# Rounding by conversion to int16 and int8, and a last batch without transfers, in a cross-attention and ternary-FFN kernel

## The chip, the cores and the metric

The kernel runs on one core of one Trainium2 chip. The metric is the device time of one execution in microseconds (us); lower is better. The kernel before is given by the median of 3 executions, and one further execution was recorded by the hardware profiler.

## The reference

The inputs are x and a context, both 32 x 128 x 512 in float32. One layer of cross attention (8 heads of 16 channels over 512 positions, with rotary embedding on half of each head) is followed by a feed-forward part (FFN) whose weights are rounded to three values and whose activations are rounded to 8 bits:

```python
def act_quant(x):                      # per token
    scale = 128 / clip(max(abs(x), axis=-1), 1e-5)
    return clip(round(x * scale), -128, 127) / scale

def weight_quant(w):                   # one scale for the whole matrix
    scale = 1.0 / clip(mean(abs(w)), 1e-5)
    return clip(round(w * scale), -1, 1) / scale

x = x + Wo @ attention(layernorm(x), ctx)          # softmax(q k / 4) v
h = layernorm(x)
z = silu(act_quant(h) @ weight_quant(w_gate).T) * (act_quant(h) @ weight_quant(w_up).T)
x = x + act_quant(fwht(z)) @ weight_quant(w_down).T  # fwht: Walsh-Hadamard over 2048
```

## The kernel before

One batch is a tile of 128 channels by 512. The 32 batches run through a software pipeline, each through these steps (the name of the step, then what it issues):

- `load`, `a`, `a2`, `a3`, `v`: x and the context come in; layer norm; projections to q, k and v on PE; the rotary part on GpSimd (POOL); q and k go through DRAM (`xd`) into the layout of the scores, `qs` and `ks` (`st`).
- `mpe`, `mdve`, `mfin`: a first product of q and k (L642, into the PSUM tile `pS`), whose row maxima are taken on VectorE (DVE, L657), transposed, and written into spare rows of `qs`.
- `epe`, `eact`, `eav`: the second, transposed product with the maxima inside it (L712, `pT`), its exponential on ScalarE (ACT, L725), and the product with v (L746, `pav`). The v tile has 16 columns of ones beside each head's 16, so `pav` holds each head's 16 outputs and 16 copies of its softmax sum.
- `u`, `o`: `pav` is copied by ACT (L769) and written to DRAM (`ud`); the sums (`sc`) and outputs (`N`) are read back, the reciprocals are made (L800), written (`rd`) and read back spread out (`RB`); N times RB (L812), the output projection (L821) and the residual (L825) give `x1`.
- `o2`: layer norm of x1, its absolute maximum, rounding to 8 bits, and a transposing DMA into `xqT` (L864).
- `gpe`, `gact`, `upe`, `udve`: gate and up products in fp8 weights (L880), SiLU (L910), product (L935).
- `bf`, `zt`, `hi`, `lo`, `hm`, `yv`: four Walsh-Hadamard stages on POOL or DVE (L964), transposes on PE (L984), and the last stages as products with a 128 x 128 Hadamard matrix in two parts (L1023, L1024), copied into `y` (L1038).
- `am`, `q`, `q1`, `q2`, `dn`: maxima of y (L1051), scaling (L1099), rounding (L1109, L1123), and the down product (L1141), the result being added to x1 (L1147) and written out.

The weights are rounded at the start by the steps `w` to `w4`: each of the three matrices comes in four tiles of 128 x 2048; absolute sums on ACT or DVE (L367), then scaling (L391), clipping (L401) and conversion to fp8 (L409). All rounding is done by adding and subtracting the constant 12582912 (`MAGIC`) in float32. For the down product, L1123 writes 127 minus the rounded value, so that a clip at zero is a clip at 127; a column sum of the weights (L418) and one more matmul of two rows (L1142, from `NEG` and `CS`) take the offset out again. The gates of the first batch wait for all twelve weight tiles (mark `wr` 2).

The order of the instructions on each engine is not written by hand. Every step is a Python generator that yields what it needs: a buffer of a ring (`get`), a mark of another step (`on`), or an engine with a planned duration. The class `Plan` plays all generators against each other when the program is built and issues, among those that can start earliest, the one of lowest rank: a number for each step in the table `CFG`, plus `T` times the batch. Where a step names two engines (as L964 does), `Plan` takes the one that ends first, with a handicap `pen` for the second. `RINGS` says how many buffers each tile has (`x1` 4, `pf` 3, `pS` and `pT` one each). On the chip each engine then runs its list in order.

Of the kernel before, what the change touches and what calls it, by code (L numbers as in the profile page):

```python
# [10 lines left out]
F32 = mybir.dt.float32  # L11
FR = mybir.dt.float32r
BF = mybir.dt.bfloat16
F8 = mybir.dt.float8e4
AF = mybir.ActivationFunctionType
# [5 lines left out]
MAGIC = 12582912.0  # L21
# [4 lines left out]
    "a": 17040.0,  # L26
    "a2": 9587.6,
    "a3": 24145.2,
    "am": 15370.4,
    "bf": 32443.0,  # L30
    "const": -13702.6,
    "dn": -12954.6,
    "eact": -26357.5,
    "eav": 10024.8,
    "epe": -25661.6,
    "gact": 12255.9,
    "gpe": 25689.6,
    "hi": 17693.4,
    "hm": -13331.7,
    "init": -13147.7,  # L40
    "lo": 14260.1,
    "load": -14103.3,
    "mdve": -26910.2,
    "mfin": -15116.6,
    "mpe": -17532.8,
    "o": -16894.5,
    "o2": -35355.2,
    "q": 9579.7,
    "q1": 31393.3,
    "q2": 30321.2,  # L50
    "st": -39068.5,
    "u": 12892.7,
    "udve": -12899.7,
    "upe": 40468.8,
    "v": 41001.5,
    "w": 11036.2,
    "w1": 23901.9,
    "w2": 38371.3,
    "w3": 34207.9,
    "w4": 33907.2,  # L60
    "yv": -12466.7,
    "zt": 12210.4,
    "T": 69.4,
    "eps": 0.025,
    "pen": 8.4,
    "stick": 7462.1,
    "epspe": 0.214,
# [5 lines left out]
    "xq": 1, "xqT": 2, "pf": 3, "z0": 2, "z1": 1, "hl": 2, "y": 1, "yq": 2, "ot": 1,  # L73
# [3 lines left out]
class Plan:  # L77

# [16 lines left out]
    def __init__(self, nc, rings, cfg):  # L95
        self.nc = nc
        self.free = dict.fromkeys(("pe", "act", "dve", "pool", "sp", "dma"), 0.0)
        self.port = {"dve": 0.0, "pool": 0.0}
        self.slots = {k: [0.0] * n for k, n in rings.items()}
        self.marks = {}  # L100
        self.tasks = []
        self.cfg = cfg
        self.now = 0.0
        self.done = 0.0
        self.eng = None
        self.table = None
        self.mode = 0
        self.locked = False
        self.tail = 0
# [11 lines left out]
    def step(self, t):  # L121
        self.now = max(t[1], t[7] + self.LAT[t[6]]) if t[6] else t[1]
        while True:
# [10 lines left out]
            t[0] = self.cfg[t[4]] + self.cfg["T"] * r[1]  # L134
# [45 lines left out]
    def run(self):  # L180
        for t in list(self.tasks):
            self.step(t)
        while True:
# [4 lines left out]
            for t in self.tasks:  # L188
# [5 lines left out]
                elif isinstance(r[0], tuple):  # L194
                    f = [(self.start(t, e), e, d) for e, d in zip(*r[:2])]
                    pen = self.cfg["pen"] if t[5] < self.tail else 0.0
# [29 lines left out]
def xattn_ffn(  # L226
# [37 lines left out]
    MAG = const.tile([128, 1], F32, name="MAG")  # L264
    nc.vector.memset(MAG, MAGIC)
    NMAG = const.tile([128, 1], F32, name="NMAG")
    nc.vector.memset(NMAG, -MAGIC)
    MAG7 = const.tile([128, 1], F32, name="MAG7")
    nc.vector.memset(MAG7, MAGIC + 127.0)
# [10 lines left out]
    CW = const.tile([128, 388], F32, name="CW")  # L280
    WQ, WK, WVT, BRP, MASK = CW[:, 0:128], CW[:, 128:256], CW[:, 256:384], CW[:, 384:386], CW[:, 386:387]
    NEGC = CW[:, 387:388]
    CM = const.tile([128, 386], F32, name="CM")
    EYE, WOT, HADF, BVO = CM[:, 0:128], CM[:, 128:256], CM[:, 256:384], CM[:, 384:386]
    ROPE = const.tile([128, 2, T], F32, name="ROPE")
    COS, SIN = ROPE[:, 0, :], ROPE[:, 1, :]
    HAD = const.tile([128, 128], FR, name="HAD")
    BO = const.tile([128, 1], F32, name="BO")
# [8 lines left out]
    ob = const.tile([128, 1], BF, name="ob")  # L297
    nc.vector.memset(ob, 1.0)
    NEG = const.tile([2, 128], BF, name="NEG")
    CS = const.tile([2, 512], BF, name="CS")  # L300

    p = Plan(nc, RINGS, CFG)
    p.tail = NB - 2
    st = [dict() for _ in range(NB)]
    NU = 2 * NB
    EARLY = 6

    def s_const():
# [6 lines left out]
        nc.scalar.copy(HAD, HADF)  # L315
        p.mark("had")
# [9 lines left out]
    def s_init():  # L326
        yield "on", "cw"
        yield "dve", 0.2
        nc.vector.tensor_scalar(NEG, ones[0:2, :], NEGC[0:2], None, ALU.mult)
# [15 lines left out]
    WR = ("z0", "z1", "z0", "y")  # L345

    def s_w():
        for n in range(12):
            m, k = divmod(n, 4)
            src = srcs[m][0][k]  # L350
            yield "get", WR[n % 4]
            yield "dma", 2.9
            w = fp.tile([128, 2048], F32, name=WR[n % 4], bufs=2 if WR[n % 4] == "z0" else 1)
            nc.sync.dma_start(out=w.rearrange("p (j i) -> p j i", j=4) if m == 2 else w, in_=src)
            WT[n] = w
            p.marks["w", n] = p.done
            p.now = p.done - 2.9

    def s_w1():
        for m in range(3):  # L360
            for n in range(4 * m, 4 * m + 4):
                yield "on", "w", n
                for h in range(2):
                    yield ("act", "dve"), (1.1, 1.13)
                    w, a = WT[n][:, bass.ts(h, 1024)], acc[:, 2 * n + h : 2 * n + h + 1]
                    if p.eng == "act":
                        nc.scalar.activation(AB, w, AF.Abs, accum_out=a)  # L367
                    else:
                        nc.vector.tensor_reduce(a, w, AX.X, ALU.add, apply_absolute_value=True)
            yield "get", "pf"  # L370
            yield "pe", 0.1
            pw = ps_f.tile([128, 512], F32, name="pf")
            nc.tensor.matmul(pw[:, 0:8], ones, acc[:, 8 * m : 8 * m + 8], start=True, stop=True)
            yield "dve", 0.1
            sw = SW[:, m : m + 1]
            nc.vector.tensor_reduce(sw, pw[:, 0:8], AX.X, ALU.add)
            p.put("pf")
            yield "dve", 0.1
            nc.vector.tensor_scalar(sw, sw, 1.0 / (NI * 128 * 512), EPS, ALU.mult, ALU.max)
            yield "dve", 0.1  # L380
            nc.vector.reciprocal(SC[:, m : m + 1], sw)
            p.mark("sw", m)

    def s_w2():
        for n in range(12):
            m = n // 4
            yield "on", "sw", m
            yield ("act", "pool", "dve"), (1.95, 2.7, 1.25), "port"
            w = WT[n]
            if p.eng == "act":  # L390
                nc.scalar.activation(w, w, AF.Identity, bias=MAG, scale=SC[:, m : m + 1])  # L391
            else:
                E[p.eng].tensor_scalar(w, w, SC[:, m : m + 1], MAGIC, ALU.mult, ALU.add)
            p.mark("w2", n)

    def s_w3():
        for n in range(12):
            yield "on", "w2", n
            yield ("dve", "pool"), (1.2, 2.7), "port"
            w = WT[n]  # L400
            E[p.eng].tensor_scalar(w, w, MAGIC - 1.0, MAGIC + 1.0, ALU.max, ALU.min)  # L401
            p.mark("w3", n)

    def s_w4():
        for n in range(12):
            m, k = divmod(n, 4)
            yield "on", "w3", n
            yield "act", 1.95
            nc.scalar.activation(srcs[m][1][:, k, :], WT.pop(n), AF.Identity, bias=NMAG, saturate=False)  # L409
            p.put(WR[n % 4])  # L410
            if k == 3:
                p.mark("wr", m)
        yield "get", "y"
        yield "get", "pf"
        yield "pe", 3.5
        pc = ps_f.tile([128, 512], F32, name="pf")
        for j in range(NI):
            nc.tensor.matmul(pc[0:1, :], ob, WDQ[:, j, :], start=(j == 0), stop=(j == NI - 1))  # L418
        yield "dve", 0.6
        w = fp.tile([128, 2048], F32, name="y")  # L420
        ca, cb = w[0:1, 0:512], w[0:1, 512:1024].bitcast(BF).rearrange("p (a f) -> p a f", a=2)
        nc.vector.tensor_scalar(ca, pc[0:1, :], 1.0 / 64.0, MAGIC, ALU.mult, ALU.add)
        yield "dve", 0.6, "port"
        nc.vector.tensor_scalar(cb[:, 0], ca, -MAGIC, None, ALU.add)
        yield "dve", 0.6, "port"
        nc.vector.tensor_scalar(ca, ca, -MAGIC, -64.0, ALU.add, ALU.mult)
        yield "dve", 0.6
        nc.vector.tensor_tensor(cb[:, 1], pc[0:1, :], ca, ALU.add)
        p.put("pf")
        yield "dma", 0.1  # L430
        nc.sync.dma_start(out=CS, in_=cb)
        p.now = p.done
        p.put("y")
        p.mark("cs")
# [324 lines left out]
    def s_u():  # L759
        for u in range(NU):  # L760
# [3 lines left out]
            yield "get", "U"  # L764
            yield "act", 0.48
# [10 lines left out]

    def s_o():
        for b in range(NB):
            s = st[b]
            yield "at", b  # L780
            yield "get", "xr"
            yield "on", "ud", 2 * b + 1
# [40 lines left out]
            yield "dve", 0.66  # L823
            x1 = x1p.tile([128, T], F32, name="x1")
            nc.vector.scalar_tensor_tensor(x1, po, BO, xr, ALU.add, ALU.add)  # L825
            p.put("pf")
            p.put("xr")
            s["x1"] = x1
            p.mark("x1", b)

    def s_o2():
        for b in range(NB):
# [18 lines left out]
            yield "get", "pf"  # L851
            yield "act", 0.75
            w = ps_f.tile([128, 512], F32, name="pf")
            nc.scalar.activation(w, l2, AF.Identity, bias=MAG, scale=sx)
            yield "dve", 0.6
            xq = xp.tile([128, T], BF, name="xq", bufs=1)
            nc.vector.tensor_scalar(xq, w, -MAGIC, 127.0, ALU.add, ALU.min)
            p.put("pf")
            p.put("l2")
# [358 lines left out]
```

## Time and profile before

| | |
|---|---|
| median of 3 executions | 1450.17 us (1441.77 to 1455.94) |
| the profiled execution | 1449.79 us, of which the span is 1447.9 us |
| granted PE clock, mean over the span | 0.950 |
| POOL L964, x489 | 616.7 us busy, 1283 ns each |
| DVE L657, x488 | 595.1 us busy, 1219 ns each |
| ACT L725, x512 | 523.0 us busy, 1022 ns each |
| PE L1142, x32 | 12.3 us busy, 384 ns each |

The profile is one execution. For each engine it gives the time in which at least one instruction was in work; matmuls are pipelined, so a busy PE need not be at its peak. The span is also cut into stretches, with the busy time of each engine and the mean clock that was granted to PE (1.00 is full). "Idle before" names what ended the idle time ahead of an instruction.

### The profile page before, as it was taken

The page shows a single profiled execution, that of the slowest core. Times are in us where ns is not written, and L with a number is a line of the kernel's source. Part 1 is how long each engine was busy: PE and PEld are TensorE (multiplying, and loading weights), DVE is VectorE, ACT ScalarE, POOL GpSimd, SP SyncE. Part 2 cuts the span into 40 slices and gives each one's busy share as a digit, 9 for nine tenths or more (in the row PEclk, how much of TensorE's full clock was granted, in tenths as well). Part 3 has the DMA queues.
Part 4 walks back from the last instruction along what each step waited for, and adds up shares of the span by engine and source line. Part 5 has one row for each costly group of instructions (what it writes and reads, how often), then busy time and mean ns, then how long its engine had stood idle before and what let it go on. Part 6 is the DMA issues. An engine that isn't in the chain of part 4 may idle for free.

```text
span 1447.9 us, 21862 instructions
## 1 busy us (share of the span) xinstructions
PE 1354.9 (94%) x7448; PEld 529.9 (37%) x7448; DVE 1173.9 (81%) x1755; ACT 1192.3 (82%) x1575; POOL 990.2 (68%) x778
## 2 busy tenths in 40 slices
PE   3797799999999999999999999999999999999965
PEld 1222233333334343333334433334333434433322
DVE  2975878888888888888888888888889888886565
ACT  5778977888988888888888888888888888888743
POOL 3112319987777878877777787887777777777830
PEclk7567999999999999999999999999999999999986
DMA  8948745454456565555445556555544555321100
GB/s 284 294 145 270 220 110 159 145 145 117 150 157 173 166 175 166 155 151 149 118 153 161 170 170 174 167 153 147 144 129 149 163 170 155 94 72 43 41 26 14
DMA packets 137699, 215.23 MB, mean 149 GB/s; under 512 B 37618, under 2 KB 39924, under 8 KB 136564
## 3 DMA queue, kind: packets, MB, share of 16 engines
q1 hardware_dynamic: 137588, 213.84, 50.4%
q8 instruction: 59, 0.97, 0.3%
q14 instruction: 52, 0.43, 0.1%
HBM read 107.35 MB, written 93.85 MB: 139 GB/s over the span
## 4 chain that ended last, share of the span: by engine, by line
PE 77%; POOL 7%; DVE 6%; ACT 5%; DMA 3%; issue 2%; SPq 0%; POOLq 0%; ACTq 0%; DVEq 0%
PE pav L746 16%; PE pf L880 13%; PE pT L712 13%; PE pS L642 9%; PE pf L1141 8%; POOL z L964 4%; PE pf L472 4%; PE pf L984 4%; PE pf L1023 3%; ACT P L725 2%; PE pf L821 2%; PE pf L552 2%; PE pf L1024 2%; DVE M L657 2%; POOL N L812 1%
## 5 line engine op out<-in xcount | busy, mean ns | idle before, releaser
L964 POOL TENSOR_TENSOR z<-z 128x512 f32<-128x512 f32 x489 | 616.7, 1283 | 103.0 <-DVE z L935 60.7
L657 DVE TENSOR_REDUCE M<-pS 128x2 f32<-128x1024 f32 x488 | 595.1, 1219 | 90.6 <-PE pS L642 89.1
L725 ACT ACTIVATE P<-pT 128x1024 f32<-128x1024 f32 x512 | 523.0, 1022 | 145.6 <-PE pT L712 144.0
L746 PE MATMUL pav<-P,va 128*32 128x512 f32 x2048 | 281.8, 623 | 0.0
L712 PE MATMUL pT<-qs,ks 50*128 50x512 f32 x1024 | 260.1, 504 | 20.8 <-ACT P L725 18.7
L642 PE MATMUL pS<-ks,qs 48*128 48x512 f32 x976 | 227.5, 457 | 12.3 <-DVE M L657 7.5
L712 PEld LDWEIGHTS pT<-qs,ks 50*128 50x128 f32 x1024 | 97.8, 187 | 242.2 <-ACT P L725 144.0
L448 POOL TENSOR_TENSOR arstd<-arstd,MHALF 128x1 f32<-128x1 f32 x32 | 18.5, 579 | 195.6 <-DVE arstd L445 160.5
L880 PEld LDWEIGHTS <-xqT 128*128 128x128 bf16 x1024 | 91.8, 99 | 155.3 <-issue 83.2
L1099 POOL TENSOR_TENSOR y<-y,YB 128x1024 f32<-128x1024 f32 x60 | 140.9, 2369 | 9.0 <-ACT YB L1085 9.0
L1141 PE MATMUL pf<-WDQ,yq 128*128 128x512 fp8e4 x512 | 127.9, 396 | 16.3 <-ACT yq L1123 16.3
L1051 DVE TENSOR_REDUCE ya<-y 128x128 f32<-128x1024 f32 x64 | 127.3, 1989 | 12.9 <-ACT y L1038 12.6
L642 PEld LDWEIGHTS pS<-ks,qs 48*128 48x128 f32 x976 | 95.9, 190 | 112.8 <-issue 43.5
L880 PE MATMUL pf<-WGQ,xqT 128*128 128x512 fp8e4 x512 | 131.4, 382 | 0.9 <-DVE ot L1147 0.5
L880 PE MATMUL pf<-WUQ,xqT 128*128 128x512 fp8e4 x512 | 126.8, 381 | 0.5 <-DVE X L525 0.2
L935 DVE TENSOR_TENSOR z<-z,pf 128x512 f32<-128x512 f32 x128 | 84.3, 675 | 17.2 <-PE pf L880 13.7
L996 ACT CAST hi<-pf 128x512 fp32r<-128x512 f32 x128 | 74.1, 586 | 26.8 <-PE pf L984 26.7
L910 ACT ACTIVATE z<-pf,tk 128x512 f32<-128x512 f32 x128 | 84.1, 684 | 8.0 <-PE pf L880 4.7
L1007 DVE TENSOR_TENSOR lo<-pf,hi 128x512 fp32r<-128x512 f32 x128 | 85.5, 675 | 3.0 <-ACT hi L996 3.0
L1141 PEld LDWEIGHTS <-yq 128*128 128x128 bf16 x512 | 46.7, 101 | 99.3 <-ACT yq L1123 27.4
L984 PE MATMUL pf<-CM,z 128*128 128x128 f32 x512 | 82.2, 285 | 0.8 <-DVE z L964 0.4
L1038 ACT COPY y<-pf 128x512 f32<-128x512 f32 x128 | 71.7, 584 | 9.5 <-PE pf L1024 9.4
(118 smaller groups left out, 1780.0 us busy)
## 6 DMA issues: line engine op xcount, KB each, us to landing
xd<-X SPq DMA_DIRECT2D x128, 512.0 KB
qs<-xd SPq DMA_DIRECT2D x128, 192.0 KB
ks<-xd SPq DMA_DIRECT2D x128, 192.0 KB
ud<-U SPq DMA_DIRECT2D x64, 256.0 KB
xt<-x SPq DMA_DIRECT2D x32, 256.0 KB
ct<-cx SPq DMA_DIRECT2D x32, 256.0 KB
RR<-R SPq DMA_DIRECT2D x64, 128.0 KB
N<-ud SPq DMA_DIRECT2D x32, 256.0 KB
```

The costliest lines, as they stand in the source:

```text
L642: nc.tensor.matmul(ps[e], qs[w, t, bass.ts(qt, 128)], ks[w, t, :], start=True, stop=True)
L657: nc.vector.tensor_reduce(m, ps[2], AX.X, ALU.max)
L712: nc.tensor.matmul(ps[:, e], ks[w, t, bass.ts(kt, 128)], qs[w, t, :], start=True, stop=True)
L725: nc.scalar.activation(P, TQ[u, n], AF.Exp, scale=0.25)
L746: nc.tensor.matmul(av[32 * h : 32 * h + 32, :], va[:, kt, 4 * hf + h, :], P[:, e], start=(kt == 0), stop=(kt == 3),)
L880: nc.tensor.matmul(ps, xqT[:, k, :], W[:, k, bass.ts(c, 512)], start=(k == 0), stop=(k == 3))
L964: E[p.eng].tensor_tensor(ix(dv, k), ix(av, 0), ix(av, 1), o)
L984: nc.tensor.transpose(ps[:, i, :], st[b]["z"][:, bass.ts(4 * c + i, 128)], EYE)
L1007: nc.vector.tensor_tensor(t, F.pop(("z", b, c)), F["hi", b, c].bitcast(F32), ALU.subtract)
L1051: nc.vector.tensor_reduce(ya[:, h], s["y"][:, 8 * h : 8 * h + 8].rearrange("p j t -> p t j"), AX.X, ALU.max, apply_absolute_value=True,)
L1099: E[p.eng].tensor_tensor(y, y, st[b]["YB"].to_broadcast([128, 8, 128]), ALU.mult)
L1141: nc.tensor.matmul(ps, s["yq"][:, j, :], WDQ[:, j, :], start=(j == 0), stop=False)
```

## The change

1. **Rounding by conversion.** A value is written to an int16 tile (activations) or int8 tile (weights), which rounds it. x: ACT writes `xi` (int16), DVE takes the minimum with 127 into bf16. y: ACT copies y into `yi` (int16), and `q2` moves from ACT to DVE, where it takes the minimum with 127. The offset of 127 goes, and with it `NEG`, `CS`, the column sum and the matmul L1142. Weights: scaling into int8 (POOL, ACT or DVE; in the built program all 14 are on POOL), then one clip on DVE that writes fp8; the steps on ACT (L391, L409) and the separate clip (L401) go.
2. **Weights in another order.** Gate and up weights first, in 10 pieces; the gates of the first batch wait for these alone (`wr` 1). The down weights come through the tile `y` one by one, twice: once for the sum, once for the rounding (8 transfers of 1 MB instead of 4). The first `dn` waits for them.
3. **The last batch** (`SHORT`). `u` takes the reciprocal of `pav` on DVE, moves it by a shuffle within groups of 32 partitions onto the outputs, and multiplies, with no DRAM; `o` is two matmuls with a padded weight `WOZ`. x is transposed by four matmuls with a bf16 identity and an ACT copy, in place of the DMA.
4. **The order.** `CFG` holds three numbers for each step, for the first 4 batches (`.h`), the last 4 (`.z`) and the rest, with new values; `pen` 42.9 instead of 8.4, `T` 295.0 instead of 69.4, `stick` 14510 instead of 7462. So all engines' lists are in a new order.

```diff
-            t[0] = self.cfg[t[4]] + self.cfg["T"] * r[1]
+            part = ".h" if r[1] < self.head else ".z" if r[1] >= self.tail else ""
+            t[0] = self.cfg.get(t[4] + part, self.cfg[t[4]]) + self.cfg["T"] * r[1]
...
+    def w_scale(w, wi, m):
+        f = w.shape[1] / 2048
+        yield ("pool", "act", "dve"), (2.6 * f + 0.1, 1.85 * f + 0.1, 1.15 * f + 0.1), "port"
+        if p.eng == "act":
+            nc.scalar.activation(wi, w, AF.Identity, scale=SC[:, m : m + 1])
+        else:
+            E[p.eng].tensor_scalar(wi, w, SC[:, m : m + 1], None, ALU.mult)
+    def w_clip(wi, o):
+        yield "dve", 1.1 * wi.shape[1] / 2048 + 0.15, "port"
+        nc.vector.tensor_scalar(o, wi, 1.0, -1.0, ALU.min, ALU.max, saturate=False)
...
+    def s_wd():
+        yield "on", "st", 1
+        for n in range(8):
+            ph, k = divmod(n, 4)
+            yield "get", "y"
+            yield "dma", 2.9
+            w = fp.tile([128, 2048], F32, name="y", bufs=1)
...
@@ s_u
+            if b in SHORT:
...
+                nc.vector.reciprocal(U, av)
...
+                nc.vector.stream_shuffle(RB, U, SWAP)
...
+                nc.vector.tensor_tensor(U, av, RB, ALU.mult)
...
@@ s_o
+                for hf in range(2):
+                    nc.tensor.matmul(po, WOZ[:, bass.ts(hf, 128)], s["U", hf], start=(hf == 0), stop=(hf == 1))
...
@@ s_o2
-            nc.scalar.activation(w, l2, AF.Identity, bias=MAG, scale=sx)
-            nc.vector.tensor_scalar(xq, w, -MAGIC, 127.0, ALU.add, ALU.min)
+            nc.scalar.activation(xi, l2, AF.Identity, scale=sx)
+            nc.vector.tensor_scalar(xq, xi, 127.0, None, ALU.min)
...
+                    nc.tensor.matmul(pt[:, k, :], xq[:, bass.ts(k, 128)], EYEB, start=True, stop=True)
...
+                nc.scalar.copy(xqT, pt)
...
@@ s_q1, s_q2, s_dn
-                nc.scalar.activation(y, y, AF.Identity, bias=MAG)
+                nc.scalar.copy(st[b]["yi"][:, w], st[b]["y"][:, w])
...
-                yield "act", 1.05
+                yield "dve", 0.42, "port"
...
-                nc.scalar.activation(s["yq"][:, w], s["y"][:, w], AF.Relu, bias=MAG7, scale=-1.0)
+                nc.vector.tensor_scalar(s["yq"][:, w], s["yi"][:, w], 127.0, None, ALU.min)
...
-            nc.tensor.matmul(ps, NEG, CS, start=False, stop=True)
```

How far the steps stand from each other is part of the change too, and can be read from the lists of the two built programs. When PE's list comes to the first L712 of batch 28, the kernel before has 26 batches of gates and 23.5 of `dn` behind it, the changed one 24 and 21. After the last L712, PE has 207 matmuls left before, 360 after. Where PE goes over from a matmul of the full array to one of half its rows (L642, L712), the list before does so 417 times, the changed one 345 times; the number of ways back (half to another form) is 568 and 570. One such turn and its price are worked out below.

## The prediction, made blind

> **What bounds the kernel now.** I read first the busy times and the clock over the span, then stretches cut at the first L712 of batches 0, 1, 2, 3, 4, 5 and 27 and at the last one, then the timeline of one steady stretch and of the end. In the page's rows the reader is to see that PE is full except at both ends, and that its clock is low in the same places:
>
> ```profile
> PE 1354.9 (94%) x7448; PEld 529.9 (37%) x7448; DVE 1173.9 (81%) x1755; ACT 1192.3 (82%) x1575; POOL 990.2 (68%) x778
> ...
> PEclk7567999999999999999999999999999999999986
> ```
>
> The stretches (us; busy PE, weight load, DVE, ACT, POOL with counts; granted clock; DMA share; GB/s) say who is full where:
>
> ```profile
> 61.00:105.00 44.00, 40.66 (x167) 13.08 (x166) 32.13 (x48) 30.52 (x37) 6.89 (x6) 0.58 0.55 186
> 105.00:145.00 40.00, 31.07 (x158) 9.37 (x154) 22.75 (x33) 35.66 (x44) 7.36 (x7) 0.79 0.83 264
> 145.00:184.00 39.00, 30.23 (x164) 10.04 (x164) 32.21 (x47) 38.60 (x42) 13.35 (x11) 0.95 0.74 217
> 184.00:233.00 49.00, 47.41 (x242) 16.26 (x242) 36.67 (x54) 34.28 (x40) 17.40 (x16) 0.94 0.38 99
> 272.00:1161.00 889.00, 886.70 (x5116) 349.31 (x5112) 774.84 (x1147) 769.10 (x1036) 708.86 (x554) 1.00 0.54 155
> 1360.00:1448.00 88.00, 56.07 (x216) 24.76 (x214) 54.40 (x91) 41.39 (x59) 25.02 (x17) 0.80 0.08 26
> ```
>
> From 272 to 1161 us (22 batches, 40.4 us each) PE is busy 99.7%: the body costs what PE's list costs. DVE is at 87%, ACT 87%, POOL 80%. From 105 to 184 ACT is the full engine (74.3 of 79 us). The last 88 us are nobody's: PE 64%, DVE 62%.
>
> **PE's list (term A).** A turn and the matmul L1142 can be priced in the timeline (start, length, engine, line):
>
> ```profile
> 712.94 1.90 PE L1141 MATMUL pf<-WDQ,yq 128*128 128x512 fp8e4 x8
> ...
> 714.77 0.50 PE L712 MATMUL pT<-qs,ks 50*128 50x512 f32 x2
> ...
> 720.40 1.90 PE L1141 MATMUL pf<-WDQ,yq 128*128 128x512 fp8e4 x8
> ...
> 722.24 0.38 PE L1142 MATMUL pf<-CS,NEG 2*128 2x512 bf16 x1
> ...
> 722.55 0.50 PE L712 MATMUL pT<-qs,ks 50*128 50x512 f32 x2
> ```
>
> Eight L1141 and then L712 take 1.83 us from start to start; with L1142 between, 2.15. So one L1142 is worth 0.32 us, 32 of them 10.2. The column sum L418 is 16 matmuls of 0.22 (their starts): 3.5, and it goes too. A turn from the full array to half of it: four L880 take 0.87 from their start to that of another full matmul (704.47 to 705.34) and 0.96 to that of L712 (700.16 to 701.12), so 0.09; the new list has 417 - 345 = 72 fewer, 6.5. The last batch adds four small matmuls and one L821 (two passes): about 1.3. A = 10.2 + 3.5 + 6.5 - 1.3 = 19 us less, nearly all of it where PE is the bound. For whole stretches I price the list by the median time between the starts of one kind of matmul and the next kind, taken between 290 and 1300 us: a body batch then costs 39.9 us, and took 40.4.
>
> **The steps moved to DVE.** Per batch DVE loses L857 (0.68) and gets two `q2` of 128x1024 and one minimum of 128x512 out of int16. No row of before reads int16. The bounds: L424, float32 to bf16 within SBUF, takes 0.41 for 512; L422, the same size out of PSUM, 0.68. So 1024 elements cost between 0.41 (should 16-bit input again halve L424's time per element) and 1.22 (L657's length for 1024). I take 0.41 to 0.68, near L424, because source and target lie in SBUF. DVE then gains 0.4 to 1.1 us a batch on the 35.2 that it has now (774.8 over 22); PE's list needs 39.5 after A's body part (0.5). DVE stays at 90 to 92%: no loss, and no gain. ACT loses L1123 (2 x 1.14) and is at 80%. The Trainium skill (VectorE: DVE Perf Modes, "The perf-mode tier table") gives 16-bit tensor-scalar work in SBUF four results per cycle and float32 two; by it the 1024 elements would be an estimated 0.43 us, and DVE's gain the lower one. No row here has shown it for int16.
>
> What speaks against it is POOL:
>
> ```profile
> 32.78 1.23 DVE L401 TENSOR_SCALAR z<-z 128x2048 f32<-128x2048 f32 x1 [2.16 <-ACT z L391]
> 32.94 2.19 POOL L580 TENSOR_TENSOR R<-R,RR 128x512 f32<-128x512 f32 x1
> ```
>
> L580 takes 1.31 on average; begun just behind a DVE L401 it took 2.19, so the DVE operation held it up for about 0.9. If each new DVE operation does the same for its whole length, POOL gets 1.1 to 1.8 us a batch on its 32.2 (708.9 over 22): 34 of 39.5. It fits, so I price it at nothing; the cover is POOL's 20% of idle time. The Trainium skill (SBUF: State Buffer, "Who interferes with whom") states the rule that this row obeys: a DVE operation in a two-port mode and a POOL operation never run together, the second one waits for the whole first. By it these operations cost POOL their full length, the case just priced.
>
> **The head (term B).** L391 and L409 take 12 x 2.09 + 12 x 2.0 = 49 us from ACT; 12 of these 24 (24.6 us) start within 105 to 184, where ACT is full. POOL gets the scaling instead: 12 tiles' worth at 2.1 (four times the memset L275 of 512, 0.53) to 4.7 us (L1099's rate, 2.37 for 1024), 25 to 57 us, in a stretch where POOL is busy 45 of 172 us (61 to 233); it queues ahead of the rotary work (L575 to L585), which feeds later batches and is not late. The gates of batch 0 no longer wait for the down weights. Four more 1 MB loads queue on SP among DMAs busy 74 to 83%. If ACT was the bound, up to 24.6 us go; if PE at its low clock is (0.58 from 61 to 105, with PE busy 92%), none. What is late next is PE: its busy time in 105 to 184, weighted by the clock, is 31.1 x 0.79 + 30.2 x 0.95 = 53 us of 79. I take 12, half of the bound.
>
> **The end (term C).** Batch 31 before, in the timeline:
>
> ```profile
> 1365.30 0.59 ACT L769 COPY U<-pav 128x512 f32<-128x512 f32 x1
> ...
> 1384.85 0.75 DVE L825 SCALAR_TENSOR_TENSOR x<-pf,BO,xr 128x512 f32<-128x512 f32 x1
> ...
> 1393.09 1.22 SPq L864 DMA_TRANSPOSE xqT<-xq  x1
> ...
> 1399.59 0.59 PE L880 MATMUL pf<-WGQ,xqT 128*128 128x512 fp8e4 x2 [0.51 <-DVE ot L1147]
> ```
>
> From `pav` to L825 it is 19.5 us, by way of DRAM. The new way is a reciprocal, a shuffle and a product, then two matmuls of two passes. The reciprocal L800 takes 0.33 for 32 elements and its form with one element 0.16, so 5.4 ns for each more: up to 2.9 us for 512, and no less than the 0.68 of other 512-element rows; I take 2.9, the same operation. With 0.7 + 0.7 + 1.9 for the rest that makes 6.2: 13 less. xqT: 6.5 us from issue to the gates, against four matmuls and an ACT copy, 0.4 + 0.59 and handovers: 5 less. So 18 us off the last batch's chain. How much of it counts? By the price of the list, PE's work behind the last L712 is 43 us before, in 88: 45 lost. The new list leaves 75 us behind it (32 shifted from the body, neutral in the sum), so there is more work to cover the chain; but that work is also DVE's and POOL's, 7 batches' `dn` with their L1051 and L964. Both bounds are open: 0 if DVE and POOL set the end, 25 if the cover is full. I take 17, the chain.
>
> **The sum.** 1449.8 (the profiled execution; the median, 1450.2, is the same) - 19 - 12 - 17 = 1402 us.
>
> **Rivals.**
> 1. *The list alone.* The head is bound by PE's low clock and the end by DVE and POOL: only A counts, 1431. For it: clock 0.58 with PE busy 92%. Against: ACT at 38.60 of 39.
> 2. *The new order stalls.* PE's list before repeats 187 matmuls with 42 turns in every batch of the body; the new one varies between 155 and 215. Of the 40.4 us 0.5 is stalls today. At 1.5, 28 more: with B and C 1430, without them 1459, which is no change.
> 3. *Slower: DVE becomes the bound.* If reading int16 runs at one element per cycle, `q2` costs 1.22, the minimum 0.68: DVE 35.2 + 2.4 = 37.6 of 39.5, 95%. Its list is strict, and L657, which frees `pS` for PE, queues behind each `q2` that waits for ACT's L1257. It decides from about 1.0 us per `q2`, where DVE passes 94%. If DVE can't be driven above 90%, a batch takes 41.8, 1.4 more than now, 39 us in 28 batches, and nothing of A but L418, nor of C, is left: 1450 - 3.5 - 12 + 39 = 1474.
>
> That the short way is not taken is excluded: the new lists hold it, once.
>
> **Chances.** A, B and C together 0.6; rival 1 0.15; rival 2 0.15 (a third of it with the gains); rival 3 0.1. What a measurement of this kernel can tell from no change is about 1%, 14.5 us. Faster by more: 0.6 + 0.15 + 0.05 = 0.80; within it 0.11; slower 0.09. The range: the full bounds of B and C (24.6 and 25) give 1381, and 9 more if the body's stalls go, 1372; upwards it takes rival 1 and stalls of 0.3 a batch more, 1440.
>
> **What would show it.** PE in the body must stay above 99% with no L1142; a body batch near 39.5 of PE's list; the length of `q2` between 0.41 and 0.68; the start of the fifth batch's L712 near 208 instead of 233 (13 of it because one batch's gates and ups, 7, half a batch of L642, 2.7, and L418, 3.5, come later or not at all); the stretch behind the last L712 near 100 us instead of 88, with PE's 75 in it. I am wrong if DVE or POOL fills the body, if a POOL scaling takes over 5 us and holds up `qs` and `ks`, or if the end takes 115.

## The result and the profile after

The changed kernel takes 1516.78 us (median; 1516.06 to 1521.76), the kernel before 1446.94 beside it: 1.048 times, 95% interval 1.042 to 1.055. 1402 was forecast, and faster. The profiled execution took 1521.76 us, its span is 1520.0.

The page's rows of the changed kernel that answer to the two shown of before:

```profile
PE 1369.6 (90%) x7406; PEld 545.8 (36%) x7406; DVE 1234.7 (81%) x1815; ACT 1082.1 (71%) x1483; POOL 1073.2 (71%) x795
...
PEclk7567979999999999999999999999999999989977
```

PE has 42 matmuls less and is busy 15 us longer in a span that is 72 us longer. ACT has lost 110 us of work, DVE and POOL have 61 and 83 more, and none of the three is above 81%. No engine has become full.

The stretches of the changed kernel, cut at its own first L809 (the old L712) of batch 5 and of batch 27 and at the last one (columns as before: stretch, length, busy PE, weight load, DVE, ACT, POOL, clock, DMA share, GB/s):

```profile
274.00:1168.00 894.00, 866.77 (x4946) 345.11 (x4945) 780.29 (x1140) 703.67 (x956) 667.75 (x518) 1.00 0.51 150
1168.00:1386.00 218.00, 204.39 (x1079) 83.10 (x1077) 171.37 (x247) 159.74 (x215) 163.73 (x124) 0.95 0.30 90
1386.00:1520.00 134.00, 91.48 (x370) 43.42 (x368) 95.31 (x157) 53.93 (x87) 77.87 (x55) 0.83 0.07 22
```

The first of these stretches is called the body here, the last one the end. In the body PE was idle for 2.3 us of 889; now it is for 27 of 894. The end has 134 us for 88, with 91 of PE in them for 56. What PE waited for in the body (engine, tile and line, what it waited for; us in all, times, longest), changed kernel:

```profile
PE pS L739 <- DVE M L754: 10.3, 21, 1.4
PE pT L809 <- ACT P L822: 9.5, 21, 1.1
```

Before, the only such row was this:

```profile
PE pf L821 <- POOL N L812: 2.1, 4, 1.0
```

Now PE comes to the scores before DVE or ACT has emptied the one buffer of `pS` or `pT`.

Priced as in the prediction, PE's list has 881 us of work between the first L712 of batch 5 and that of batch 27 before, and took 889; the new one has 840 (FFN work has been put off until later) and took 894. By this estimate stalls of 8 us have become 54, 2.45 a batch; 27 of the 54 are PE's idle time above, the other 27 lie within its busy time (867 us for a list of 840). The whole list became 16 us shorter, from 1279 to 1263, where term A had 19; the time lost beside it went from 169 to 257 us. In the table, the last column counts the gate matmuls (16 a batch) that are still to come after the last scores:

| first scores of batch (us) | 0 | 4 | 5 | 27 | last | end | gate matmuls left |
|---|---|---|---|---|---|---|---|
| before | 61 | 233 | 272 | 1161 | 1360 | 1448 | 28 |
| changed | 70 | 225 | 274 | 1168 | 1386 | 1520 | 60 |

So of 72 us, 2 had been lost at batch 5, 7 at batch 27, 26 at the last scores, and 46 come behind them. In the stretch from batch 27 to the last scores the granted clock fell as well. Before, it was 1.00 there:

```profile
1161.00:1360.00 199.00, 193.91 (x1075) 78.59 (x1071) 156.21 (x231) 168.28 (x224) 153.50 (x118) 1.00 0.36 100
```

Now it is 0.95, and about as many matmuls (1079) keep PE busy for 204 us instead of 194; that is half of the 19 us lost there. No run separates this from the stalls that come with it.

The end is not idle for want of one engine. Its chain (start, length, piece; changed kernel) lies on POOL from 1410.66 to 1428.86, and then hands the work round between ACT, PE, DVE and POOL:

```profile
1432.63 0.72 ACT xi L987
1433.98 2.76 PE pf L1024 x12
1436.77 0.69 DVE z L1079
1441.14 2.36 POOL y L1243
1443.52 1.05 ACT yi L1257
1444.60 1.48 DVE yq L1274
1446.13 3.59 PE pf L1292 x8
```

Three costs could lie behind the whole loss: the operations put on DVE, which wait for POOL; the weights' scaling on POOL; and the order. The groups of the changed kernel (busy us, mean ns of one):

```profile
L1274 DVE TENSOR_SCALAR yq<-yi 128x1024 bf16<-128x1024 int16 x64 | 54.2, 859 | 18.5 <-ACT yi L1257 18.4
L991 DVE TENSOR_SCALAR xq<-xi 128x512 bf16<-128x512 int16 x32 | 22.1, 691 | 2.1 <-ACT xi L987 2.1
...
L867 DVE RECIPROCAL U<-pav 128x512 f32<-128x512 f32 x2 | 6.7, 3358 | 2.5 <-PE pav L843 2.5
L870 DVE STREAM_SHUFFLE RB<-U 128x512 f32<-128x512 f32 x2 | 1.5, 737 | 0.0
```

The mean of L1274 hides two kinds. In the timeline of the changed kernel, the first here has POOL idle, and the pair below begins while POOL is in L1108:

```profile
627.75 0.42 DVE L1274 TENSOR_SCALAR yq<-yi 128x1024 bf16<-128x1024 int16 x1
...
739.11 4.12 POOL L1108 TENSOR_TENSOR z<-z 128x512 f32<-128x512 f32 x3
...
739.43 2.67 DVE L1274 TENSOR_SCALAR yq<-yi 128x1024 bf16<-128x1024 int16 x2
...
742.02 1.21 DVE L754 TENSOR_REDUCE M<-pS 128x2 f32<-128x1024 f32 x1
```

The 12 that began with POOL idle took 0.418 us on average (0.40 to 0.43). The 52 with a POOL operation in flight took 0.96, up to 1.61, and most ended 0.28 to 0.29 us after that operation. This waiting of a DVE operation for a POOL operation in flight is called the lock below. L754, which empties `pS`, stands behind them.

### The profile page after: what moved, and what is told of

It reads as the page before. It is cut to its first block, busy times and chain, and to the rows that moved or that the text cites. A ratio compares the mean times of both kernels' runs of the same rounds, so it can differ in the third digit from the quotient of the medians.

```text
span 1520.0 us, 21799 instructions
## 1 busy us (share of the span) xinstructions
PE 1369.6 (90%) x7406; PEld 545.8 (36%) x7406; DVE 1234.7 (81%) x1815; ACT 1082.1 (71%) x1483; POOL 1073.2 (71%) x795
## 4 chain that ended last, share of the span: by engine, by line
PE 52%; DVE 22%; POOL 7%; DMA 7%; ACT 7%; issue 5%; SPq 1%; ACTq 0%; POOLq 0%; DVEq 0%
PE pav L843 10%; PE pf L1024 10%; PE pT L809 9%; DVE M L754 8%; PE pS L739 7%; PE pf L1292 6%; ACT P L822 4%; DVE ya L1195 3%; PE pf L569 2%; POOL yi L466 2%; POOL z L1108 2%; PE pf L1128 2%; DMA xd<-X 2%; DVE yq L1274 2%; PE pf L961 2%
## 5 line engine op out<-in xcount | busy, mean ns | idle before, releaser
L1108 POOL TENSOR_TENSOR z<-z 128x512 f32<-128x512 f32 x491 | 624.4, 1293 | 106.1 <-DVE z L1079 72.0
L754 DVE TENSOR_REDUCE M<-pS 128x2 f32<-128x1024 f32 x488 | 594.7, 1219 | 118.5 <-PE pS L739 116.4
L809 PE MATMUL pT<-qs,ks 50*128 50x512 f32 x1024 | 260.5, 505 | 36.4 <-ACT P L822 35.4
L843 PE MATMUL pav<-P,va 128*32 128x512 f32 x2048 | 286.3, 629 | 1.9 <-ACT U L882 1.6
L739 PE MATMUL pS<-ks,qs 48*128 48x512 f32 x976 | 233.6, 470 | 43.2 <-DVE M L754 32.5
L809 PEld LDWEIGHTS pT<-qs,ks 50*128 50x128 f32 x1024 | 99.0, 190 | 289.4 <-ACT P L822 187.6
L1243 POOL TENSOR_TENSOR y<-y,YB 128x1024 f32<-128x1024 f32 x60 | 140.9, 2371 | 52.8 <-ACT YB L1229 52.8
L569 PE MATMUL pf<-ct,CW 128*32 128x512 f32 x256 | 77.0, 674 | 1.4 <-DVE lo L1151 1.2
L1128 PE MATMUL pf<-CM,z 128*128 128x128 f32 x512 | 78.2, 284 | 0.1
```

The lines of the kernel that those rows point to most:

```text
L569: nc.tensor.matmul(ps[64 * dh + 32 : 64 * dh + 64, :], WK[:, w], ct, start=True, stop=True)
L739: nc.tensor.matmul(ps[e], qs[w, t, bass.ts(qt, 128)], ks[w, t, :], start=True, stop=True)
L754: nc.vector.tensor_reduce(m, ps[2], AX.X, ALU.max)
L809: nc.tensor.matmul(ps[:, e], ks[w, t, bass.ts(kt, 128)], qs[w, t, :], start=True, stop=True)
L843: nc.tensor.matmul(av[32 * h : 32 * h + 32, :], va[:, kt, 4 * hf + h, :], P[:, e], start=(kt == 0), stop=(kt == 3),)
L1108: E[p.eng].tensor_tensor(ix(dv, k), ix(av, 0), ix(av, 1), o)
```

## The experiments

Each changes the kernel named. Ratios are to the kernel before, measured on the same chip, with their 95% intervals; it took 1446 to 1449 us on each of them, so times of different runs are also set side by side. "Order kept" means that every engine's list is the same but for the operations named. In the expectations, "order theory" lays the loss on the new lists whatever the operations are, and "operations theory" on the new operations whatever the order is.

**e1, e2: ranks and program crossed.**

```diff
e1, changed kernel:   CFG, T, pen, stick: those of before
e2, kernel before:    CFG, T, pen, stick, the .h and .z ranks: those of the changed kernel
```

> The changed kernel (int16/int8 rounding, last batch without transfers) with the step ranks, T, pen and stick of the kernel before; the ranks have no separate values for the first and last batches. If the new order is the cause (PE stalls of 2 us a batch in the body and 134 us behind the last pT product), this falls back to 1400 to 1440 us, with the body at 40 us a batch or less and under 100 us behind the last pT product. If the rounding steps on DVE, which wait for POOL, are the cause, it stays above 1480. If both, 1440 to 1480.

> The kernel before (rounding by a large constant, offset matmul, last batch through DRAM) with the step ranks, T, pen and stick of the changed kernel, separate for the first 4 and last 4 batches. If the order is the cause: 1490 us or more, again with a body of unequal batches and a long end. If the rounding is the cause: 1430 to 1460. If the order suits only the durations it was made for, it is slower than both.

1538.9 (1.061, 1.054 to 1.068) and 1544.9 (1.066, 1.060 to 1.071). Both bodies take 42.0 us a batch, both ends over 125 us. Neither set of ranks belongs to the old or the new rounding as such; a set gives a good list only with the program and the planned durations it stands with, and these two runs do not yet tell order from operations.

**e3: without the short way.**

```diff
-    SHORT = (NB - 1,)
+    SHORT = ()
```

> The changed kernel with the last batch through DRAM and the transposing DMA like all others. If the short way shortens the end as I priced it: 10 to 18 us slower than the changed kernel, 1527 to 1535. If DVE and POOL set the end, within 5 us of it, 1512 to 1522. If the two 3.36 us reciprocals hurt, faster by up to 7.

1514.4 (1.045, 1.031 to 1.058): part 3 of the change brings nothing that can be measured. The interval, of two executions, is as wide as the gain that was forecast; in the profiled execution the end takes 132 us without the short way, against 134 with it.

**e4: the minima taken out, order kept.** It leaves out the rounding and clipping of x and y: ACT writes bf16, and each minimum is cut to one element per partition.

```diff
-                nc.vector.tensor_scalar(s["yq"][:, w], s["yi"][:, w], 127.0, None, ALU.min)
+                nc.vector.tensor_scalar(s["yq"][:, w, 0:1], s["yq"][:, w, 0:1], 127.0, None, ALU.min)
```

> The changed kernel in exactly its order on every engine, but ACT writes x and y as bf16 without rounding and the DVE minima with 127 shrink to one element a partition (activations are not rounded; the weights are). This takes 76 us of DVE time away. If the waits of these minima for POOL, and the time they hold DVE, are the cause: the body falls to 38.5 to 39.3 us a batch and the whole to 1440 to 1475. If the order is the cause whatever DVE does: above 1500.

1501.9 (1.036, 1.032 to 1.040). The minima, with their waits for POOL, cost about 15 us of the 70; the rest stays, just on the order's side of the expectation. In the body, PE's waits for `pS` behind L754 fall from 10.3 us to 4.6. The end is still 132 us.

**e5, e6: another order for the same program.** Two random searches over the ranks, started from those of before, with planned durations corrected to the measured ones.

```diff
-        yield ("pool", "act", "dve"), (2.6 * f + 0.1, 1.85 * f + 0.1, 1.15 * f + 0.1), "port"
+        yield ("pool", "act", "dve"), (5.35 * f + 0.1, 2.0 * f + 0.1, 1.15 * f + 0.1), "port"
...
+CFG: from the search
```

> The changed program whole, with another set of ranks (a search of the planner's own list of ranks, started from the ranks of the kernel before, against planned durations of the POOL scaling, the reciprocal and the x rounding that are set to the measured 5.6, 3.4 and 0.7 us). If the order is what cost the time: the body falls from 40.6 to about 39.5 us a batch (PE list 38.2 plus some stalls), the last scores come near 1350 and the end near 1440 to 1465, a ratio of 0.99 to 1.01. If the operations of the change cost it (waits of the minima behind POOL, the slow POOL scaling of the weights, VectorE's greater load): whatever the order, 1500 or more, ratio 1.035 or above, with the body at 40.3 or above.

> The same, with the ranks of a second search from the same start that took another path. Order theory: within 15 us of e5, so 1430 to 1475, and the same reading of the stages (body near 39.5, fewer FFN matmuls left behind the last scores than the 220 of the changed kernel). Operations theory: 1500 or more. If one searched order is fast and the other is not, single orders scatter by that much and only the best of them tells the change's worth.

1466.8 (1.012, 1.009 to 1.015) and 1473.7 (1.018, 1.014 to 1.022): 43 to 50 us come back with every operation of the change in place. e5 lies 2 us above the order theory's numbers, e6 within them, and both far below the other theory's 1500. The reading of the stages was wrong all the same: the body is no better (41.3 us a batch in e5), but only 32 gate matmuls are left behind the last scores and the end takes 81 us. The end of e5:

```profile
1385.00:1466.00 81.00, 54.10 (x228) 26.05 (x226) 61.62 (x99) 33.53 (x53) 35.69 (x25) 0.83 0.04 15
```

**e7, e8: one part alone in the old order (kept).**

```diff
e7, kernel before
-            nc.tensor.matmul(ps, NEG, CS, start=False, stop=True)
e8, kernel before
-            nc.scalar.activation(w, l2, AF.Identity, bias=MAG, scale=sx)
+            nc.scalar.activation(xi, l2, AF.Identity, scale=sx)
```

> The kernel before, its order kept on every engine, without the 32 offset matmuls of L1142; leaves out the offset's correction, so the output is 128 times the weights' column sums too high before scaling. Term A of the forecast (PE's list is the bound, each instruction taken from it shortens the end by its duration): 10.2 us off, 1437, ratio 0.993. If PE's list is not the bound of the end (waits for other engines absorb it): no change, ratio 1.000.

> The kernel before, its order kept on every engine, with only the rounding of x changed: ScalarE writes int16 to SBUF instead of fp32 with the magic number to PSUM, and VectorE's minimum reads that. Lock theory (a VectorE operation from SBUF to SBUF waits for the POOL operation in flight): the 32 minima take 0.5 to 0.9 us in place of 0.3 to 0.4, delays of at most 0.6 us each that a body without stalls hides, ratio 0.998 to 1.006. If the order of this program stands on such small delays: up to 0.6 us a batch, ratio up to 1.013.

e7: 1437.1 (0.9935, 0.9911 to 0.9959), 9 us less, for 10.2 forecast. Here, in a body nearly without stalls, the matmuls taken from PE's list were worth their price. e8: 1446.9 (1.0006, 0.998 to 1.003): 32 minima out of int16 cost nothing here.

**e9 to e12: the change step by step in the old order.** Each operation stands where the one it replaces stood (e12's ranks are the old ones too, but its lists move in the last two batches). In e10, e11 and e12 two int8 tiles are used in turn and some are overwritten before they are clipped, so some weight tiles hold another tile's values; the instructions and their sizes are those of the rounding.

```diff
e9   x as in e8; ACT: y -> int16, DVE: min(127) -> bf16 (at L1109, L1123); no L418, no L1142
e10  e9; w2 -> int8 on ACT, w3 -> clip int8 to fp8 on DVE, w4 empty
e11  e10; w2 on POOL
e12  e10; SHORT = (NB - 1,)
```

> The change's rounding of x and y put into the kernel before, instruction for instruction, in its own order on every engine: x by int16 as in e8, y written by ScalarE as int16 and clipped by 64 minima that take the place of 64 ScalarE passes but stand on VectorE, no offset sum and no offset matmuls. Order theory: the roundings are harmless, the time is e7's 1437 less up to 3 us for the 16 matmuls of L418 and plus up to 4 us for stalls of VectorE, so 1433 to 1441, ratio 0.991 to 0.997. Operations theory (VectorE fills with 64 minima of 0.96 us, 1.9 us a batch, and each waits for POOL): the body grows from 40.0 to 41 us a batch or more, ratio 1.01 or above.

> As e9, and the weights by int8 too, again in the places of the old passes: the scaling on ScalarE (as it stood before), the clip int8 to fp8 on VectorE, the third pass of ScalarE over the 12 weight tiles (24 us in all) gone. If ScalarE or VectorE sets the head: first scores up to 5 us earlier, ratio 0.986 to 0.995. If PE's own list and the loads set it: the same as e9 within 3 us.

> As e10, but all 12 scalings on POOL, as the changed kernel has them (5.6 us each, 67 us in all, between the rotary work of batches 0 to 5). If the slow scaling cost the changed kernel its 9 us in the head: first scores at 66 to 72 us in place of 59 to 61, the fifth batch's first scores some 5 to 10 us later than in e10, and the end 4 to 10 us later, ratio to e10 about 1.005. If the order is all of it: no later than e10 by more than 3 us.

> As e10, with the last batch's short way added (reciprocal, shuffle and product on VectorE, x transposed by PE): all the parts of the change, with the ranks of before, so that the order moves only in the last two batches. The forecast's term C: 17 us off the end, so about 0.985 of e10. If the end is bound by the FFN work left behind the last scores, as e3 had it: within 5 us of e10.

e9: 1437.6 (0.994, 0.991 to 0.997), the same as e7: 96 minima on DVE, in exchange for 64 passes of ACT and the column sum, cost nothing on balance. e10: 1433.2 (0.991, 0.988 to 0.994). e11: 1461.4 (1.011, 1.007 to 1.015), 28 us more than e10, where 10 was the most expected. e12: 1440.6 (0.995, 0.993 to 0.997), 7 more than e10, where term C has 17 less; the end takes 87.7 us with the short way and 87.5 without it. POOL at the start of e11:

```profile
29.35 11.93 POOL L397 TENSOR_SCALAR yi<-z,SC 128x2048 int8<-128x2048 f32 x2 [7.67 <-DVE SC L384]
41.26 1.26 POOL L569 TENSOR_TENSOR R<-R,ROPE 128x512 f32<-128x512 f32 x1
```

and of the changed kernel:

```profile
28.19 10.87 POOL L466 TENSOR_SCALAR yi<-z,SC 128x2048 int8<-128x2048 f32 x2 [4.99 <-DVE SC L457]
39.03 2.23 POOL L672 TENSOR_TENSOR R<-R,ROPE 128x512 f32<-128x512 f32 x1
```

A tile takes 5.45 us in the median, up to 6.5, and the rotary work of batch 0, which began at 30.4 before, waits behind two of them. In e11 the fifth batch's first scores come at 252 us (e10 231) and nothing later makes it good.

**e13 to e16: the new order with its costs taken out (order kept).**

```diff
e13  changed kernel:  w_scale on ACT in place of POOL
e14  e5:              w_scale on ACT in place of POOL
e15  e10:             each int8 tile in its own place (no tile shared)
e16  e4 and e13 together
```

> The changed kernel, its order kept on every engine, with the 14 int8 scalings written by ScalarE (about 2 us for 2048) at the places where POOL had them (5.6 us). If POOL's scaling holds up the changed kernel as it held up e11 (28 us for 12 tiles): first scores at 61 to 64 instead of 70 and the end 15 to 28 us earlier, 1490 to 1502, ratio 1.03 to 1.037. If the order alone makes the loss: the head's 6 to 9 us at most come back and are lost again in waits, 1507 to 1520, ratio 1.042 or above.

> e5 (the searched order), the scalings on ScalarE in the same way. If e5's rest over the old order is POOL's scaling: 1440 to 1452, ratio 0.995 to 1.003. If it is the order (its body took 41.3 us a batch, 1.5 above e10's): 1455 to 1467, ratio 1.005 or above.

> e10 with each int8 tile written into the first quarter of its own fp32 tile, so that no tile is shared. Same instructions, same order, the same waits but for the shared buffers: e10's 1433 within 4 us, ratio 0.988 to 0.994.

> e4 and e13 together: the changed kernel's order, scalings on ScalarE, ScalarE writes bf16 unrounded and the minima are cut to one element per partition (leaves out the rounding and clipping of x and y). If the three causes add: e4 took 15 us off, e13 takes x off, so 1517 - 15 - x; what is left over e10's 1433 is the order's own price. Order as main cause: 1478 to 1495, so 45 to 60 us left. If minima and scaling are the main cause: below 1465.

e13: 1504.5 (1.041, 1.038 to 1.044), 12 us off, between the two expectations. The scaling on POOL is a cost, about as large as that of the minima. e14: 1477.7 (1.022, 1.017 to 1.026), 11 us slower than e5 and outside both expectations: taking the scaling off POOL did not bring e5 to the time of the old order. Why the same work on ACT made it slower no run shows; that ACT's list was not laid out for it is a guess. e15: 1433.6 (0.991, 0.989 to 0.994), so e10's shared tiles had not mattered for its time. e16: 1488.0 (1.028, 1.025 to 1.031): the two costs add (15 and 12; together 29).

In e16 neither the minima nor the scaling on POOL are left, and it is still 54 us above e15, which has the minima too. The two bodies and ends, e16 first, then e15:

```profile
257.00:1139.00 882.00, 862.86 (x4948) 344.30 (x4949) 743.29 (x1140) 702.02 (x956) 660.44 (x518) 1.00 0.52 152
1139.00:1352.00 213.00, 201.74 (x1075) 82.16 (x1073) 159.31 (x247) 159.13 (x214) 161.98 (x124) 0.95 0.32 92
1352.00:1484.00 132.00, 92.65 (x371) 44.80 (x370) 87.77 (x157) 54.23 (x88) 76.87 (x55) 0.83 0.07 23
```

```profile
268.00:1152.00 884.00, 881.39 (x5097) 347.88 (x5095) 789.75 (x1193) 725.44 (x991) 714.93 (x555) 1.00 0.55 156
1152.00:1350.00 198.00, 191.67 (x1068) 77.81 (x1065) 160.94 (x241) 157.75 (x213) 154.77 (x118) 1.00 0.36 100
1350.00:1436.00 86.00, 54.38 (x213) 24.51 (x211) 59.80 (x100) 32.00 (x51) 24.78 (x17) 0.82 0.08 27
```

e16's body takes as long as e15's with 149 matmuls fewer in it; its next stretch takes 15 us more, and its end, with what the body put off, 46 more. e16 was 11 us ahead at batch 5. These parts make 48 (-2, 15, 46, and -11 for the head), the difference of the two spans.

e16 also keeps two other parts that e15 has not: the weights in their new sequence, with four more loads, and the short way. The first cannot be the 54, since e16 stands ahead at batches 4 and 5 (210 against 230 us, 257 against 268). The second made -2 us (e3, within its wide interval it could be nearly 20 either way) and +7 (e12); e12's narrower interval leaves it far below 54.

## Why the prediction was wrong

**The step that failed is the premise of the sum**, "the body costs what PE's list costs", carried over to a list that is not the old one. Term A took the shorter list for a shorter time. The list did become 16 us shorter, but of the lists measured here only those in the old order have a body nearly free of stalls. Rival 2 names this mechanism; it was given 0.15 and "1.5, 28 more", and the stalls took 54 us in place of 8 (2.45 a batch), 42 of them the order's own: e16 has the same PE list, hence the same 840 us of work, in 882. The front part of the document already had the sign of it: 24 batches of gates behind PE at the first scores of batch 28 in place of 26.

**Minima: "no loss, no gain"** held in the old order (e9 against e7, 0.5 us) and cost about 15 in the new one (e4). Their own length was right: 0.418 us for 1024, the low end of 0.41 to 0.68. The lock was read in one direction only: POOL held up by DVE. The other way costs more here, since DVE's next operation can be the one that frees `pS`: the minimum took 0.96 us with POOL in flight, and PE's waits for `pS` fell by more than half in e4. Whether a minimum of y meets POOL is a matter of order: 52 of 64 did in the changed kernel, 9 of 64 in e15:

```profile
L1119 DVE TENSOR_SCALAR yq<-yi 128x1024 bf16<-128x1024 int16 x64 | 31.0, 485 | 2.1 <-ACT yi L1105 2.1
```

The Trainium skill (SBUF: State Buffer, "Who interferes with whom") gives the lock for both directions; both kernels agree with it, and 0.41 us free against 0.94 to 0.96 held up is its price here.

**Term B, 12 us gained.** "2.1 to 4.7" for a scaling on POOL was too low: 5.45. That is over 5 us, which the prediction named as a sign of being wrong. "Not late", said of the rotary work, was wrong too: e13 puts the cost at 12 us, and the first scores come at 61 with the scaling on ACT, at 70 with it on POOL. With it on ACT (e13) the fifth batch's first scores come at 207, where 208 was forecast, so the rest of the head's reckoning may have been near; but e13 has also put off FFN work that before had done by then, and its end pays for that. On its own, the rounding of the weights without ACT's third pass makes about 4 us (e10, e15 against e9), which the overlapping intervals do not tell from nothing.

**Term C, 17 us gained** for the short way: the chain's terms were near (reciprocal 3.36 for 2.9, shuffle 0.74, product 0.69 for 0.7), yet e3 shows no gain and e12 a loss of 7. "32 shifted from the body, neutral in the sum" was the wrong step: the body did not give the 32 back (41 us less of list, 5 us longer), and behind the last scores the shifted work is not PE's alone. 134 us were needed there for a list of 75, 59 of them gaps where before there were 45: in the chain above each piece goes from PE to DVE, POOL, ACT and back, and the end has no other batches' scores to fill the gaps. The prediction's own mark of failure, an end of 115, was passed.

**What held**: L1142 at 0.32 us each (10.2 forecast, 9 in e7); DVE not the bound (87% of the body, where 90 to 92 were forecast), so rival 3 did not happen; the granted clock as before in the body. ACT's "80%" comes to 83 by the prediction's own terms (769.1 over 22, less 2 x 1.14, of 39.5) and was 79; nothing rested on it.

The answer to what the change is worth: in the old order its rounding is faster than before by 0.9% (e15, 0.6 to 1.1), and no version here whose rounding is whole is faster. It leaves out part 3 and the new weight sequence and keeps the scaling on ACT. In the order it was given, the whole change is 4.8% slower.

What stays open is why the new ranks fall behind with the FFN. In the trace of the changed kernel the time from the end of a batch's `pav` to its x1 grows from 31 us (batch 1) to 107 (batch 25), where e15 has 28 throughout the body (27 to 29); and from x1 to L1297 it takes 147 to 189 us up to batch 25, where e15 takes 136 in the body. There are four buffers of x1, each held from L893, which writes it, to L1297. The ring is full in the changed kernel: in batches 5 to 21 a buffer is written again 1.3 to 10 us after it comes free, 2.9 in the median, where the kernel before and e15 have 23. Batch 14 makes room for 18 in the changed kernel, then 11 for 15 in the kernel before:

```profile
928.00 0.75 DVE L1297 SCALAR_TENSOR_TENSOR ot<-pf,yc,x 128x512 f32<-128x512 f32 x1 [0.42 <-PE pf L1292]
...
930.88 0.75 DVE L893 SCALAR_TENSOR_TENSOR x<-pf,BO,xr 128x512 f32<-128x512 f32 x1 [0.41 <-PE pf L961]
```

```profile
722.66 0.75 DVE L1147 SCALAR_TENSOR_TENSOR ot<-pf,yc,x 128x512 f32<-128x512 f32 x1 [0.92 <-PE pf L1142]
...
747.21 0.75 DVE L825 SCALAR_TENSOR_TENSOR x<-pf,BO,xr 128x512 f32<-128x512 f32 x1 [1.33 <-PE pf L821]
```

A buffer is held for 168 us on average there, so four of them let one batch through every 42, while scores come every 40.6; before it is 137 us, one batch every 34. This would explain why the FFN never catches up. e16 has the same (166 us held, 2.9 in the median), so neither the minima nor POOL's scaling makes it. It is not the whole of the matter: e6's body is slow too (41.6) with 27 us between. No run gave x1 a fifth buffer, and why the new ranks hold each buffer 30 us longer stays open.

## What to carry to other kernels

An order fixed when the program is built is a part of the kernel like any operation: price a change of the operations and a change of the order apart, above all by putting the new operations where the old ones stood; here that showed a gain that the new order had hidden. A shorter list on the full engine is a gain only where its waits stay as they were, so look first at how far each batch's later steps lag behind, and at what is left when the full engine's cover ends. And an operation that is cheap alone may wait for a neighbour, so ask what stands behind it on its engine.

## What the hardware showed that was not expected

- A tensor-scalar operation of 128 x 2048 from float32 to int8 takes 5.45 us on POOL (median of the changed kernel). ACT does the same in 2.0 (e15). For each element POOL is slower at this than at its product of two float32 tensors (L1243, 1024 elements in 2.37).
- DVE's minimum out of int16 runs at 0.418 us for 1024 elements and 0.285 for 512 (six of the 32 L991 that had POOL idle) and, with POOL in flight, ends 0.28 and 0.15 us after POOL's operation.
- DVE's reciprocal of 128 x 512 takes 3.36 us, five times its product of the same size (0.69).
